# Moving the attention's projections from the first stage of a graph layer into its gather stage

## The chip, the core and the metric

One core of a Trainium2 chip runs the whole program. The metric is the device time of one execution in microseconds (us), and the time given for a kernel is the median of its runs. The engines are TensorE (PE in the profile, with PEld for its weight loads), VectorE (DVE), ScalarE (ACT), GpSimd (POOL) and SyncE (SP), which issues plain transfers.

## The reference, cut to what matters

The layer works on 6250 nodes with 256 features and 206,250 edges (100,000 in both directions and one self loop for each node). It adds a graph attention, a linear attention over all nodes and a mixture of eight experts. The linear attention is the part that the change touches:

```python
xn = _layernorm(x)                                   # (6250, 256)
# linear attention: rmsnorm, projection, softmaxes, context, output
qkv = rmsnorm(xn, g_pre) @ w_qkv                     # w_qkv (256, 384)
q, k, v = to_heads(split(qkv))                       # 4 heads of 32 features
k = concatenate([mem_kv[0], k]); v = concatenate([mem_kv[1], v])
q = softmax(q, over the features of a head) * SCALE
k = softmax(k, over all nodes)
context = einsum('bhdn,bhen->bhde', k, v)
out = einsum('bhde,bhdn->bhen', context, q)
mix = rmsnorm(out @ w_out + b_out, g_out) + xn
# graph attention: x@W; e = exp(leaky(el[src] + er[dst])); sums over src of e * (x@W)[dst]
gnn = elu(sums / rowsums + b)
x = x + gnn + mix
x = x + moe(_layernorm(x))                           # 8 experts, two of them weighted for each node
```

Since the softmax of the keys runs over all nodes, the context (128 by 128, by heads) is ready only when every node has been projected, and the outputs of the linear attention can follow only after it.

## The kernel before

The nodes are cut into 49 tiles of 128 rows (`NT`), in 13 groups of four (`groups`; the last group has one tile). All data are float32 unless said.

**First stage.** For each group `project(t0, n)` loads the rows (`xt`), takes mean and variance on ACT, normalises (`xn`, L338), transposes the tile on PE (`tp`, L343), copies it back on ACT (`xT`, L345) and multiplies it with `wcat`, which holds the columns for q, k, v and for the graph table side by side, 456 in all (L348, output `pr`). ACT then copies q out into `q_all` (L351), k and v into `kv` (L352) and 72 columns into `tab` (L355); these go to the graph table in DRAM (`table`). Behind each group stand three calls of `sort_batch`, of 51 in all, which sort the edges by source. A batch counts on PE (`n_ps`, L395), scans on DVE (L399), makes ranks on PE (`r_ps`, L419 and L420), reads them with a reduction on DVE (L427), builds one-hot rows on DVE (`ohp`, L448; `rv`, L444) and multiplies them on PE (`g_ps`, L454).

When the projections are done, `context()` runs between the remaining batches: one reduction on DVE over all keys finds the maximum (`kmax`, L468), POOL subtracts it from the keys (L498), ACT takes the exponentials (L499), and PE sums keys times values over 49 tiles (L502). At its end stands `cw`, the context times `w_out`.

**Gather stage.** `pack(q)` makes, for two tiles at a time, the list of edge targets in order (`dst_x`, L951; its heavy steps are `ohc` L923, `rc` L930, `ohp` L935 on DVE and `s_ps` L940 on PE). For each tile `gather` then issues 35 indirect transfers on POOL (L972), each of 128 table rows, into one of three buffers `xe`. A tile's gather may start when the tile three before it has been summed. The sums are `weights` (`z`, L1018 to L1029; exponentials `ew`, L1031) and four calls of `sums`, each with one wide product on DVE (`ohw`, L1041) and some eleven matmuls on PE (`a_ps`, L1048). `look` prepares the one-hot rows of the next tile (L984, L997, ACT copy `ohT` L1001, L1009).

Other work is placed between these by a list `todo` of generators with a cost for each of their steps, of which `some_more` takes a share four times a tile. At first the list holds the outputs of the linear attention, 39 steps for 13 groups, at two units a step:

```python
todo = [(attention(), [FC] * (3 * len(groups)))]        # FC = 2
```

In `attention()` each group takes the softmax of q (DVE L583, L584, L586 to L588, ACT L585), then for each tile a transpose on PE (L594), a copy on ACT (L596), a matmul with `cw` (256 columns, L598), an addition on DVE (L599) and a square on ACT (L601); at last the norm, a second load of `x` and the sum, stored to `base_y` in DRAM (L603 to L620). A block's four calls of a tile take at most two units each, so the 39 steps are spread over the first ten tiles. When they are done the experts' weights are loaded, and each block of four tiles that has been summed puts its `finish_steps` on the list: L681 to L764 and the experts, `h_ps` (512 columns, L775), Gelu (L783), `y_ps` (256 columns, L791) and the weighted sum on DVE (L795).

Within these bounds the order of each engine's instructions is fixed when the program is built, by a scheduler that follows the program's order and the buffers; each engine works its list in order. `later(ins)` ties an instruction behind the first `dst_x`, so that it is not moved ahead of it. In the gather stage PE's outputs other than the sums share two PSUM buffers (`y_ps`) and one of 512 columns (`h_ps`).

Of the kernel before, what the change touches and what calls it, by code (L numbers as in the profile page):

```python
# [1 line left out]

# [15 lines left out]
P = 128  # L18
# [17 lines left out]
def tile_gps_layer(  # L36
# [53 lines left out]
    KW = 2 * HID + 1  # L90
    O_TAB = 3 * HID
    O_EL = O_TAB + H + FO
    PW = O_EL + H
    assert NPAD > N and PW <= 512 and last > 0
# [141 lines left out]
    with tc.tile_pool(name="ids", bufs=1) as lp:  # L236
# [21 lines left out]
    nc.scalar.dma_start(out=wcat[:, :, :3 * HID], in_=w_qkv.rearrange("(c p) f -> p c f", p=P))  # L258
    nc.scalar.dma_start(
        out=wcat[:, :, O_TAB + H:O_EL], in_=gnn_W.rearrange("(c p) f -> p c f", p=P)  # L260
    )
# [3 lines left out]
    gpre = kp.tile([P, DC], F32, name="gpre")  # L265
# [5 lines left out]
    wo = kp.tile([P, D], F32, name="wo")  # L271
    nc.scalar.dma_start(out=wo, in_=w_out)
    mk = kp.tile([P, NM], F32, name="mk")
    nc.scalar.dma_start(out=mk, in_=mem_kv[0].rearrange("h d m -> (h d) m"))
    mv = kp.tile([P, NM], F32, name="mv")
# [6 lines left out]
    for c in range(DC):  # L282
        wt_ps = mps.tile([FO, P], F32, name="tp")
        nc.tensor.transpose(wt_ps, wcat[:, c, O_TAB + H:O_EL], ident)
        wT = qw.tile([FO, P], F32, name="wT")
        nc.scalar.copy(wT, wt_ps)
        wlr_ps = mps.tile([P, 2 * H], F32, name="pr")
        nc.tensor.matmul(wlr_ps, lhsT=wT, rhs=lrT, start=True, stop=True)
        nc.scalar.copy(wcat[:, c, O_TAB:O_TAB + H], wlr_ps[:, :H])
        nc.scalar.copy(wcat[:, c, O_EL:PW], wlr_ps[:, H:])  # L290
        nc.vector.tensor_scalar(
            wcat[:, c, :3 * HID], wcat[:, c, :3 * HID], gpre[:, c:c + 1], None, op0=OP.mult
        )

    q_all = qp.tile([P, NT, HID], F32, name="q_all")
    kv = kp.tile([P, NT, KW], F32, name="kv")
    nc.gpsimd.memset(kv[:, :, KW - 1:KW], 1.0)
    kmax = kp.tile([P, HID], F32, name="kmax")

    def xn_of():  # L300
        return qw.tile([P, D], F32, name="xn")

    def project(t0, n):
# [10 lines left out]
        for j in range(n):  # L314
# [8 lines left out]
        rn = qw.tile([P, GT], F32, name="rn")  # L323
        nc.scalar.activation(rn[:, :n], var, AF.Sqrt, scale=float(D))
        nc.vector.tensor_mul(rn[:, :n], rn[:, :n], rs)
        nc.vector.tensor_scalar_max(rn[:, :n], rn[:, :n], 1e-12)
        nc.vector.reciprocal(rn[:, :n], rn[:, :n])
        nc.vector.tensor_scalar_mul(rn[:, :n], rn[:, :n], float(D) ** 0.5)
        shift = qw.tile([P, GT], F32, name="shift")
        nc.vector.scalar_tensor_tensor(  # L330
            shift[:, :n], stats[:, t0:t0 + n, 0], -1.0, rs, op0=OP.mult, op1=OP.mult
# [3 lines left out]
        for j in range(n):  # L335
# [3 lines left out]
                xn, xt[:, j, :], AF.Identity, bias=shift[:, j:j + 1], scale=rstd[:, t:t + 1]  # L339
# [7 lines left out]
            for c in range(DC):  # L347
# [3 lines left out]
            nc.scalar.activation(q_all[:, t, :], pr[:, :HID], AF.Copy, scale=rn[:, j:j + 1])  # L351
            nc.scalar.activation(  # L352
                kv[:, t, :2 * HID], pr[:, HID:3 * HID], AF.Copy, scale=rn[:, j:j + 1]
            )
            nc.scalar.copy(tab[:, j, :], pr[:, O_TAB:PW])  # L355
# [110 lines left out]

    def context():
        nc.vector.tensor_reduce(  # L468
            kmax, kv[:, :NT - 1, :HID].rearrange("p t d -> p d t"), axis=AX.X, op=OP.max
        )  # L470
        nc.vector.tensor_max(kmax[:last], kmax[:last], kv[:last, NT - 1, :HID])
        km_ps = mps.tile([HID, P], F32, name="tp")
        nc.tensor.transpose(km_ps, kmax, ident)
        kcol = kp.tile([P, 2], F32, name="kcol")
        nc.vector.tensor_reduce(kcol[:, 0:1], km_ps, axis=AX.X, op=OP.max)
        nc.vector.tensor_reduce(kcol[:, 1:2], mk, axis=AX.X, op=OP.max)
        kmc = kp.tile([P, 1], F32, name="kmc")
        nc.vector.tensor_max(kmc, kcol[:, 0:1], kcol[:, 1:2])
        kr_ps = mps.tile([P, HID], F32, name="tp")
        nc.tensor.transpose(kr_ps, kmc.to_broadcast([P, P]), ident)  # L480
        krow = kp.tile([P, HID], F32, name="krow")
        nc.vector.tensor_copy(krow, kr_ps)
        nkm = kp.tile([P, 1], F32, name="nkm")
        nc.vector.tensor_scalar_mul(nkm, kmc, -1.0)
        emk = kp.tile([P, NM], F32, name="emk")
        nc.scalar.activation(emk, mk, AF.Exp, bias=nkm)
        mm_ps = mps.tile([NM, 2, P], F32, name="tp")
        nc.tensor.transpose(mm_ps[:, 0, :], emk, ident)
        nc.tensor.transpose(mm_ps[:, 1, :], mv, ident)
        memT = kp.tile([NM, 2, P + 1], F32, name="memT")  # L490
        nc.vector.memset(memT, 1.0)
        nc.vector.tensor_copy(memT[:, :, :P], mm_ps)
        ctx_ps = mps.tile([P, HID + 1], F32, name="pr")
        nc.tensor.matmul(ctx_ps, lhsT=memT[:, 0, :P], rhs=memT[:, 1, :], start=True, stop=False)
        yield
        for t0, n in groups:
            kk = kv[:, t0:t0 + n, :HID]
            nc.gpsimd.tensor_sub(kk, kk, krow[:, None, :].to_broadcast([P, n, HID]))  # L498
            nc.scalar.activation(kk, kk, AF.Exp)  # L499
            for t in range(t0, t0 + n):  # L500
                rows = P if t < NT - 1 else last
                nc.tensor.matmul(  # L502
                    ctx_ps, lhsT=kv[:rows, t, :HID], rhs=kv[:rows, t, HID:KW],
                    start=False, stop=(t == NT - 1),
                )
            yield
        rden = kp.tile([P, 1], F32, name="rden")
        nc.vector.reciprocal(rden, ctx_ps[:, HID:HID + 1])
        nc.vector.tensor_scalar_mul(rden, rden, float(DH) ** -0.5)
        cbd = kp.tile([P, HID], F32, name="cbd")  # L510
        nc.vector.memset(cbd, 0.0)
        for h in range(MH):
            s = slice(h * DH, (h + 1) * DH)
            nc.vector.tensor_scalar(cbd[s, s], ctx_ps[s, s], rden[s], None, op0=OP.mult)
        cT_ps = mps.tile([P, HID], F32, name="tp")
        nc.tensor.transpose(cT_ps, cbd, ident)
        cT = kp.tile([P, HID], F32, name="cT")
        nc.scalar.copy(cT, cT_ps)
        cw_ps = mps.tile([P, D], F32, name="pr")
        nc.tensor.matmul(cw_ps, lhsT=cT, rhs=wo, start=True, stop=True)  # L520
        nc.scalar.copy(cw, cw_ps)
        yield

# [20 lines left out]
    steps = context()  # L544
    while batches:
        sort_batch(batches.pop(0))
        next(steps, None)
    for _ in steps:
        pass
# [17 lines left out]
    def later(ins):  # L567

        tc.add_manual_dep(
            ins.ins, gate[0].ins.name,  # L570
            mybir.DependencyInfo(mybir.DependencyClass.NoSync, mybir.DependencyReason.DATA),
        )

    def attention():
# [4 lines left out]
        for t0, n in groups:  # L579
# [10 lines left out]
            o_g = qw.tile([P, GT, D], F32, name="o_g")  # L590
            ss = qw.tile([P, GT], F32, name="ss")
            for j in range(n):
# [7 lines left out]
                sq = qw.tile([P, D], F32, name="sq")  # L600
# [455 lines left out]
    todo = [(attention(), [FC] * (3 * len(groups)))]  # L1056
# [207 lines left out]
```

## Time and profile before

| | |
|---|---|
| median of 3 runs | 4222.5 us (4214.7 to 4229.85) |
| profiled execution, its own time | 4182.5 us |
| its span | 4180.7 us |
| busy in the span: PE, PEld, DVE, ACT, POOL | 54%, 40%, 46%, 18%, 40% |
| mean granted clock of TensorE | 0.711 |
| first gather issued, last gather issued | 446.2 us, 3993.6 us |
| gathers of one tile (35 indirect transfers) | 44 us on POOL, tile after tile, 49 tiles |

The profile is of one execution, and its times are counted from the start of the span. In a row of the windows view the first pair is the window, then its length, then for each engine the busy time and in brackets the number of instructions, then the granted clock of TensorE as a share of full speed, the busy share of the DMA engines and their rate. In a row of a group the first number behind the bar is the busy time, the second the mean of one instruction in ns; overlapping matmuls make the busy time less than count times mean. Behind "<-" stands what ended a wait. "Remote" means that the profile knows a semaphore's wait but not the instruction that ended it.

### The profile page before, as it was taken

The page shows a single profiled execution, that of the slowest core. Times are in us where ns is not written, and L with a number is a line of the kernel's source. Part 1 is how long each engine was busy: PE and PEld are TensorE (multiplying, and loading weights), DVE is VectorE, ACT ScalarE, POOL GpSimd, SP SyncE. Part 2 cuts the span into 40 slices and gives each one's busy share as a digit, 9 for nine tenths or more (in the row PEclk, how much of TensorE's full clock was granted, in tenths as well). Part 3 has the DMA queues.
Part 4 walks back from the last instruction along what each step waited for, and adds up shares of the span by engine and source line. Part 5 has one row for each costly group of instructions (what it writes and reads, how often), then busy time and mean ns, then how long its engine had stood idle before and what let it go on. Part 6 is the DMA issues. An engine that isn't in the chain of part 4 may idle for free. (4 is left out here: it accounts for less than half of the span.)

```text
span 4180.7 us, 39357 instructions
## 1 busy us (share of the span) xinstructions
PE 2268.6 (54%) x15401; PEld 1663.9 (40%) x15401; DVE 1919.8 (46%) x3941; ACT 746.2 (18%) x1653; POOL 1669.8 (40%) x1774
## 2 busy tenths in 40 slices
PE   7877232435254764644765555455364573554677
PEld 4544232324242543433543433334253352442456
DVE  7787444536352443533442523425343452342423
ACT  5542001212111111111111110111111111110122
POOL 1001545454445344344344344544535335344410
PEclk8875555666666877776877776777676686776778
DMA  1020111111121111011011100101101001011100
GB/s 59 28 29 1 21 28 41 37 41 37 34 74 20 22 19 23 18 24 22 12 29 18 25 17 17 30 17 22 25 12 27 18 19 25 13 25 19 23 12 7
DMA packets 106548, 103.75 MB, mean 25 GB/s; under 512 B 42678, under 2 KB 78740, under 8 KB 106356
## 3 DMA queue, kind: packets, MB, share of 16 engines
q0 software_dynamic: 54720, 60.52, 8.4%
q1 hardware_dynamic: 49940, 39.75, 3.3%
q8 instruction: 123, 2.02, 0.2%
q10 hardware_dynamic: 1696, 0.89, 0.1%
q14 instruction: 69, 0.57, 0.0%
HBM read 86.39 MB, written 14.65 MB: 24 GB/s over the span
## 5 line engine op out<-in xcount | busy, mean ns | idle before, releaser
L972 POOL DMA_INDIRECT xe<-table,dst_x x1710 | 1635.7, 957 | 2011.0 <-PE a_ps L1048 1323.2
L1048 PE MATMUL a_ps<-ohw,xe 128*65 128x128 f32 x4400 | 665.1, 307 | 235.7 <-issue 189.3
L1048 PEld LDWEIGHTS a_ps<-ohw,xe 128*65 128x65 f32 x4400 | 590.8, 159 | 314.4 <-issue 243.1
L775 PE MATMUL h_ps<-tokT,w1s 128*128 128x512 f32 (+3 forms) x896 | 442.8, 610 | 235.1 <-ACT hT L783 205.1
L795 DVE SCALAR_TENSOR_TENSOR x<-y_ps,comb,x 128x256 f32<-128x256 f32 x392 | 187.0, 481 | 782.4 <-remote 479.1
L791 PE MATMUL y_ps<-w2s,hT 128*128 128x256 f32 x1568 | 436.7, 413 | 147.6 <-issue 107.2
L791 PEld LDWEIGHTS y_ps<-w2s,hT 128*128 128x128 f32 x1568 | 315.5, 208 | 273.0 <-issue 177.5
L940 PE MATMUL s_ps<-rc,ohp 128*128 128x144 f16 x2525 | 255.1, 260 | 279.5 <-DVE ohp L935 146.8
L1041 DVE TENSOR_TENSOR ohw<-oh,bank 128x1280 f32<-128x1280 bf16 x196 | 321.5, 1641 | 170.1 <-remote 149.3
L940 PEld LDWEIGHTS <-ohp 128*128 128x128 f16 x2525 | 209.6, 114 | 324.2 <-DVE ohp L935 162.9
L1009 PE MATMUL e_ps<-elw,ohT 128*128 128x48 bf16 x588 | 36.2, 199 | 544.7 <-ACT ohT L1001 477.8
L783 ACT ACTIVATE hT<-h_ps,b1s 128x512 f32<-128x512 f32 (+3 forms) x224 | 140.4, 627 | 1018.4 <-remote 531.0
L775 PEld LDWEIGHTS h_ps<-tokT,w1s 128*128 128x128 f32 x896 | 171.8, 214 | 345.7 <-ACT hT L783 226.0
L1001 ACT COPY ohT<-t_ps 128x768 bf16<-128x768 bf16 x98 | 78.3, 799 | 1130.1 <-remote 842.3
L930 DVE TENSOR_TENSOR rc<-ohc,bank 128x1152 f16<-128x1152 f16 (+1 forms) x350 | 231.2, 687 | 64.8 <-remote 62.2
L1009 PEld LDWEIGHTS <-ohT 128*128 128x128 bf16 x588 | 27.0, 106 | 577.2 <-ACT ohT L1001 505.9
L935 DVE TENSOR_TENSOR ohp<-to,bank 128x2048 f16<-128x2048 f16 (+1 forms) x175 | 193.5, 1105 | 0.0
L763 PE MATMUL y_ps<-b2s,cTs 8*128 8x256 f32 x98 | 49.7, 600 | 192.4 <-ACT cTs L761 118.6
L764 DVE TENSOR_TENSOR x<-x,y_ps 128x256 f32<-128x256 f32 x49 | 20.6, 420 | 269.7 <-remote 164.6
L1018 DVE TENSOR_REDUCE z<-e_ps 128x140 f32<-128x420 f32 (+1 forms) x49 | 28.7, 585 | 244.6 <-PE e_ps L1009 224.1
L923 DVE TENSOR_TENSOR ohc<-to,bank 128x1152 f16<-128x1152 f16 (+1 forms) x175 | 119.6, 683 | 0.3 <-ACT to L911 0.2
L448 DVE TENSOR_TENSOR ohp<-rank,iota_h 128x4096 f16<-128x4096 f16 (+1 forms) x51 | 116.1, 2277 | 6.3 <-ACT rank L439 6.0
(273 smaller groups left out, 2568.0 us busy)
## 6 DMA issues: line engine op xcount, KB each, us to landing
xe<-table,dst_x POOLq DMA_INDIRECT x1710
xt<-in_x_dram SPq DMA_DIRECT2D x24, 512.0 KB
base_y<-xt SPq DMA_DIRECT2D x12, 512.0 KB
yt<-base_y SPq DMA_DIRECT2D x9, 512.0 KB
out_dram<-x SPq DMA_DIRECT2D x9, 512.0 KB
w1s<-in_L_ffn_w_dram SPq DMA_DIRECT2D x8, 256.0 KB
w2s<-in_L_ffn_w_dram SPq DMA_DIRECT2D x8, 256.0 KB
table<-tab SPq DMA_DIRECT2D x12, 138.0 KB
```

The source lines that it names most:

```text
L448: nc.vector.tensor_tensor(pairs(ohp[:, :w]), two(rank2[:, :w], P // 2), row(iota_h, P // 2), op=OP.is_equal)
L775: nc.tensor.matmul(h_ps[:, :w], lhsT=w1s[:, e, c, f * P:(f + 1) * P], rhs=held["tokT"][:, c, :w], start=(c == 0), stop=(c == DC - 1),)
L783: nc.scalar.activation(held[e][:, f, :w], h_ps[:, :w], AF.Gelu, bias=b1s[:, k:k + 1])
L791: nc.tensor.matmul(y_ps, lhsT=held[e][:, f, j * P:(j + 1) * P], rhs=w2s[:, e, f, :], start=(f == 0), stop=(f == FC - 1),)
L795: results.append(nc.vector.scalar_tensor_tensor(x2[:, j, :], y_ps, held["comb"][:, j, e:e + 1], x2[:, j, :], op0=OP.mult, op1=OP.add,))
L923: nc.vector.tensor_tensor(pairs(ohc[:, :m]), twos(to[:, 0, t0:t0 + m], U * CW // 2), iota_2[:, :, :U * CW // 2].to_broadcast([P, m, U * CW ...
L930: nc.vector.tensor_tensor(pairs(rc[:, :m, i, :]), pairs(ohc[:, :m]), twos(edges_q[:, t0:t0 + m, i, :], U * CW // 2), op=OP.mult,)
L935: nc.vector.tensor_tensor(pairs(ohp[:, :m]), twos(to[:, 1, t0:t0 + m], P // 2), iota_2.to_broadcast([P, m, P // 2, 2]), op=OP.is_equal,)
L940: nc.tensor.matmul(flat(s_ps), lhsT=ohp[:, t - t0, :], rhs=flat(rc[:, t - t0]), start=(t == 0), stop=(t == NBT - 1),)
L972: nc.gpsimd.indirect_dma_start(out=xe[:, c, :], out_offset=None, in_=table, in_offset=bass.IndirectOffsetOnAxis(ap=dst_x[:, c:c + 1], axis=0),
L1041: nc.vector.tensor_tensor(ohw[:, :n], oh[:, g0:g1, i, None, :].to_broadcast([P, n, H, SN]), ew_s[:, c0:c0 + n, :, None].to_broadcast([P, n ...
L1048: nc.tensor.matmul(a_ps[:, i].rearrange("f h n -> f (h n)"), lhsT=xe[:, c, H:], rhs=ohw[:, c - c0].rearrange("p h n -> p (h n)"), start=(c ...
```

## The change

The first stage keeps only what the table needs. `wcat` shrinks to 72 columns, `project` copies out `tab` alone, and `context()` is taken out of the first stage; the sort batches that stood among its steps follow one another. What belongs to the linear attention becomes a new `context()` in the gather stage, which stands in `todo` ahead of `attention()`: 41 steps and 39 steps, each now at one unit, so that a call takes two of them.

For each group of four tiles the new `context()` loads `x` again (the load for the next group is issued one step ahead), normalises (ACT), transposes (PE) and copies back (ACT) into `xnT`, 512 nodes wide; makes the keys by feature, `k_ps` with 128 features by 512 nodes (PE); takes the group's maximum for each feature (DVE) and updates a running maximum, with a factor `shrink` for what was summed before; takes the exponentials (ACT); makes q and v by tile, 256 columns (PE, two copies on ACT); transposes the exponentials back (PE, one copy on ACT); sums keys times values of the group in PSUM and adds the sum to `sums_c` (DVE). The weights for q, k, v and a few small tensors move from the pool that is closed after the first stage into the one that stays open until the attention is done, and two buffers of `attention()` (`o_g`, `sq`) are cut to a single copy.

```diff
-    nc.scalar.dma_start(out=wcat[:, :, :3 * HID], in_=w_qkv.rearrange("(c p) f -> p c f", p=P))
+    wqvk = qp.tile([P, DC, 3, HID], F32, name="wqvk")
+    for i, k in enumerate((0, 2, 1)):
+        nc.scalar.dma_start(out=wqvk[:, :, i], in_=w_qkv[:, k * HID:(k + 1) * HID]...)
...
     def project(t0, n):
...
-        nc.vector.tensor_mul(rn[:, :n], rn[:, :n], rs)
-        nc.vector.tensor_scalar_max(rn[:, :n], rn[:, :n], 1e-12)
-        nc.vector.reciprocal(rn[:, :n], rn[:, :n])
-        nc.vector.tensor_scalar_mul(rn[:, :n], rn[:, :n], float(D) ** 0.5)
...
-            nc.scalar.activation(q_all[:, t, :], pr[:, :HID], AF.Copy, scale=rn[:, j:j + 1])
-            nc.scalar.activation(
-                kv[:, t, :2 * HID], pr[:, HID:3 * HID], AF.Copy, scale=rn[:, j:j + 1]
-            )
-            nc.scalar.copy(tab[:, j, :], pr[:, O_TAB:PW])
+            nc.scalar.copy(tab[:, j, :], pr)
...
-    steps = context()
     while batches:
         sort_batch(batches.pop(0))
-        next(steps, None)
...
+    def context():
...
+        for g, (t0, n) in enumerate(groups):
+            v = vs[g % 2]
+            xnT = qw.tile([P, DC, GT * P], F32, name="xnT", bufs=1)
+            for j in range(n):
+                t = t0 + j
+                xn = xn_of()
+                nc.scalar.activation(xn, xt[:, j, :], AF.Identity, bias=shift_all[:, t:t + 1],
+                    scale=rn_all[:, t:t + 1])
+                xT_ps = yps.tile([P, DC, P], F32, name="y_ps")
+                for c in range(DC):
+                    nc.tensor.transpose(xT_ps[:, c, :], xn[:, c * P:(c + 1) * P], ident)
+                nc.scalar.copy(xnT[:, :, j * P:(j + 1) * P], xT_ps)
+            if g + 1 < len(groups):
+                xt = load(g + 1)
+            yield
+            k_ps = hps.tile([P, GT * P], F32, name="h_ps")
+            for c in range(DC):
+                nc.tensor.matmul(k_ps[:, :w], lhsT=wqvk[:, c, 2], rhs=xnT[:, c, :w], ...)
+            here = small("here")
+            nc.vector.tensor_reduce(here, k_ps[:, :w], axis=AX.X, op=OP.max)
+            new = small("most")
+            nc.vector.tensor_max(new, most, here)
+            less = small("less")
+            nc.vector.tensor_scalar_mul(less, new, -1.0)
+            shrink = small("shrink")
+            nc.scalar.activation(shrink, most, AF.Exp, bias=less)
+            most = new
+            ekT = qw.tile([P, GT * P], F32, name="ekT", bufs=1)
+            nc.scalar.activation(ekT[:, :w], k_ps[:, :w], AF.Exp, bias=less)
+            for j in range(n):
+                qv_ps = yps.tile([P, 2, HID], F32, name="y_ps")
+                for c in range(DC):
+                    nc.tensor.matmul(flat(qv_ps), lhsT=xnT[:, c, j * P:(j + 1) * P],
+                        rhs=flat(wqvk[:, c, :2]), ...)
+                nc.scalar.copy(q_all[:, t0 + j, :], qv_ps[:, 0])
+                nc.scalar.copy(v[:, j, :HID], qv_ps[:, 1])
+            yield
+            for j in range(n):
+                nc.tensor.transpose(ek_ps[:r, j, :], ekT[:, j * P:j * P + r], ident)
+            nc.scalar.copy(ek[:r, :n], ek_ps[:r, :n])
+            for j in range(n):
+                nc.tensor.matmul(c_ps, lhsT=ek[:r, j, :], rhs=v[:r, j, :], ...)
+            nc.vector.scalar_tensor_tensor(sums_c, sums_c, shrink, c_ps, op0=OP.mult, op1=OP.add)
+            yield
...
-    todo = [(attention(), [FC] * (3 * len(groups)))]
+    todo = [(chain(context(), attention()), [1] * (6 * len(groups) + 2))]
```

## The prediction, made before the changed kernel ran

> **What bounds the kernel now.** I read the windows view first, by stage, then the waits of the gather stage, then groups and single instructions for prices.
>
> ```profile
> core 0: us, PE busy (x) PEld busy (x) DVE busy (x) ACT busy (x) POOL busy (x), PEclk, DMA share, GB/s
> 86.80:284.40 197.60, 175.35 (x2044) 103.85 (x2041) 152.87 (x252) 116.49 (x449) 2.86 (x18) 0.81 0.11 33
> 284.40:410.00 125.60, 83.48 (x1132) 57.97 (x1132) 104.66 (x128) 26.34 (x86) 19.32 (x15) 0.61 0.12 3
> 558.80:1099.00 540.20, 218.04 (x1472) 179.37 (x1470) 262.47 (x537) 79.28 (x185) 272.74 (x281) 0.64 0.17 38
> 1306.40:3893.20 2586.80, 1410.92 (x8215) 1033.72 (x8216) 1064.42 (x2268) 367.07 (x546) 1133.03 (x1190) 0.73 0.11 21
> 640.20:666.60 26.40, 0.00 (x0) 0.00 (x0) 0.00 (x0) 0.00 (x0) 15.89 (x17) 0.50 0.17 24
> ```
>
> Row 1 is the projections among 27 sort batches, row 2 the context among the last 16: PE and DVE are both nearly full. Row 3 is gather tiles 2 to 9, where the change puts its work, row 4 tiles 13 to 46. Row 5 is a piece of one tile: only POOL's gathers run, PE, DVE and ACT do nothing at all.
>
> ```profile
> POOL xe L972 <- PE a_ps L1048: 1302.9, 43, 51.4
> ```
>
> This is from the waits between 600 and 3900 us: 43 times POOL waits, 30.3 us each, until PE has summed the tile three before. So a tile is serial: 35 gathers (43.4 to 45.7 us), about 5.5 us until the other engines move again, and then what is left of the tile's work. The others get 9 to 25 us of work done early in a burst and then stand still until its end. Work added here is therefore paid, though PE is idle 60% of row 3. Tiles 2 to 9 take 67.5 us each with PE 27.3 and DVE 32.8 busy; tiles 13 to 46 take 76.1 with 41.5 and 31.3. So 8.6 us of time stand against 14.2 us more PE, 0.60 for one. A least-squares fit over tiles 3 to 47 gives 41.5 + 0.57 PE + 0.35 DVE (rms 3.8 us); with ACT as a third term 43.0 + 0.54 PE + 0.17 DVE + 0.48 ACT (rms 3.6). I use the first.
>
> **First stage: what goes.** The first gather is issued at 446.2. Sort batch starts (`ohp` L448) are at 36.6, 86.8 (8th), 284.4 (35th) and 410.0 (51st, a short one of about 3.1 us): 373.4 us in all. With projections a batch takes 197.6/27 = 7.32 us; without, 6.0 (at 300 to 324 us) to 6.92 (four batches from 378 us, clock 0.50).
>
> ```profile
> L348 PE MATMUL pr<-wcat,xT 128*128 128x456 f32 x196 | 109.8, 690 | 5.9 <-ACT xT L345 5.9
> L351 ACT ACTIVATE q_all<-pr,rn 128x128 f32<-128x128 f32 x49 | 17.8, 364 | 47.2 <-PE pr L348 47.0
> L468 DVE TENSOR_REDUCE kmax<-kv 128x128 f32<-128x6144 f32 x1 | 11.0, 11044 | 0.0
> L498 POOL TENSOR_TENSOR kv<-kv,krow 128x512 f32<-128x512 f32 x12 | 18.6, 1586 | 41.1 <-DVE krow L482 41.1
> ```
>
> These groups lie in 0 to 440 us. The 456-column matmuls become 72 columns wide: 109.8 us become about 39, bounded by their 196 weight loads at some 200 ns. ACT loses L351 (17.8) and L352 (22.9), DVE the 11.0 of `kmax`, POOL the 18.6, PE the 17.9 of L502. While POOL subtracts, DVE's L444 takes 1.25 to 1.56 us where it had taken 0.58:
>
> ```profile
> 328.58 0.58 DVE L444 TENSOR_TENSOR rv<-ob,vb 128x832 f16<-128x832 f16 x1
> 337.88 1.56 DVE L444 TENSOR_TENSOR rv<-ob,vb 128x832 f16<-128x832 f16 x1
> ```
>
> So 49 pitches plus 3.1 us: at 6.0 us 297 (76 saved), at 6.35 314 (59 saved), at 6.92 342 (31 saved). DVE alone needs 152.87/27 = 5.66. I take 6.35, between: tables and statistics still stand among three quarters of the batches, but PE falls from 6.5 us a batch to about 4. First stage: -59.
>
> **Gather stage: what comes.** Prices are from the groups between 446 and 1100 us, nearest in place and kind:
>
> ```profile
> L598 PE MATMUL y_ps<-cw,qT 128*128 128x256 f32 x82 | 37.0, 541 | 50.3 <-ACT qT L596 44.6 <-issue 4.4 <-DVE ohw L1041 0.7
> L594 PE MATMUL y_ps<-ident,q_all 128*128 128x128 f32 x41 | 13.7, 334 | 1.6 <-DVE q_all L588 1.6
> ```
>
> - PE: 147 transposes (98 of `xn`, 49 of `ekT`) at 13.7/41 = 0.334 make 49 us (36 at the first stage's 0.247); 52 k matmuls of 512 columns as L775 (442.8/896 = 0.494) 26; 196 q/v matmuls of 256 columns at 37.0/82 = 0.451 make 88 (55 at L791's 436.7/1568 = 0.279); 98 of the context at 0.185 (L502) 18. Together 181, at the low prices 135; I take 158, for PE will be busier here than now but less than where L791 stands.
> - DVE: 13 maxima of 512 columns at 0.675 (as L583) 8.8, 26 small operations at 0.17 4.4, 13 additions to `sums_c` at 0.3 3.9, beginning and end about 5: 22.
> - ACT: 49 normalisations at 0.606, 49 copies of 256 columns at 0.385, 98 of 128 columns at 0.264, 13 exponentials and 13 copies of 512 columns at about 0.6, 13 of `shrink` at 0.2: 93.
>
> Two-engine fit: 0.57·158 + 0.35·22 = 98. Three-engine fit: 0.54·158 + 0.17·22 + 0.48·93 = 134. The two first bursts have nothing to sum, so about one group of 13 (8 us) is done there for nothing: 90 and 126. I take 100, nearer the two-engine one, since ACT runs in chains with PE and is idle 85% of row 3.
>
> [...] The granted clock is 0.81 where the projections stand now (row 1), 0.64 where they go (row 3) and 0.50 in the frozen piece (row 5), and a 256-column matmul takes 0.451 us between the gathers of row 3 against 0.279 among the experts' runs. With every price at its high end the sum is 0.57·23 = 13 us above mine, with every one at its low end 13 below. [...]
>
> **What is moved or added and priced at nothing.** Attention keeps its instructions but runs in tiles 5 to 9 alone at double rate: about 13 us of DVE more a tile there, 13 less in tiles 0 to 4; the fit is linear, so the sum is zero. If the lighter tiles can't fall as the heavier ones rise, it costs up to 5·13·0.35 = 23. From about tile 11 on the order of every engine's instructions is as before. Thirteen more loads of `x` (512 KB, on SP's queue among attention's loads and stores, one step ahead) are 6.3 MB; SP's queue moved 39.75 MB in 3.3% of the span, so they take about 22 us of the engines' time, in some 330 us at a DMA share of 0.17; uncovered at most 22. POOL's queue holds the same gathers and loses only the subtractions. New waits: DVE's maximum waits for PE's k, and behind it in DVE's list stand `pack`'s steps and `z`; ACT's copies wait for PE's transposes, and behind them stand `ohT` and `ew`; transposes, q/v and sums all take turns in the two `y_ps` buffers, each freed only by a copy on ACT or DVE. If each of 39 steps holds up a tile's chain by 0.5 us, that is 20; zero if the next tile's `ohw` waits anyway. This is inside 90 to 126.
>
> **Sum.** -59 + 100 = +41. The profiled execution took 4182.5 us (span 4180.7), which gives 4223.5. The median of 4222.5 is 40 above the profiled time, so the same step on it gives 4263.5, rounded to 4263. A difference of 0.3% (13 us) is about what a measurement of this kernel can tell from no change.
>
> **Rivals.**
> - *Faster, 4182 (0.20).* PE's idle time takes the work. For: PE is idle 322 of 540 us in row 3, and the early part of a burst has 9 to 25 us in which engines do run; bursts 0 to 2 have little to sum. If gather growth is 20 us and the first stage gives 61, -41. It decides where growth over the ten tiles stays under about 59 us, 6 a tile: at the fit's 0.57 some 70 of the 158 us on PE (41/0.57) would have to be hidden beyond what the fit hides already. Against: row 5, and the 30.3 us wait that ends with PE.
> - *Much slower, 4317 (0.20).* With less PE work in the first stage its clock stays at 0.50 and the pitch at 6.92 (-31), while ACT and PE exchange halves at each step so that the three-engine fit holds (+126): +95. For: the four 6.92 batches stand where no context is left. Against: their POOL and table work is different from the earlier batches'.
> - *No difference, near 4222 (0.10).* Growth equals saving, say 65 against 65.
> - That the change doesn't do what it says can be left out: in the new order of PE's instructions 24 of 98 transposes and 16 q/v matmuls stand among the first tile's sums, and no 456-column matmul is left.
>
> **Numbers.** Likeliest 0.50 of slower by 20 to 70; with the much slower case that makes slower by over 0.3% 0.70, within 0.3% 0.10, faster by over 0.3% 0.20. The likeliest case's own range is 4235 to 4290 (pitch 6.0 to 6.6, growth 85 to 115). The whole range, leaving a tenth at each end, is 4190 to 4325: half of the faster case lies below it, and half of the much slower one, 8 us of waits on top of it, above.
>
> **What the changed profile would show.** The first gather issued near 387 us (right if 370 to 415; if over 415, the pitch is the failed step). Batches at about 6.35 us with DVE busy 5.7 of it. Tiles 2 to 4 and 5 to 9 at about 75 to 80 us instead of 67.5, their PE busy 16 us higher, clock 0.64 or more. Tiles from 13 on at 76 as before. The context's matmuls should lie mostly between the end of a burst and the next one's start; if they lie early in bursts and POOL's wait for L1048 stays 30 us or less, the faster rival is right. If the late waits name DVE's maximum or SP's loads, my zero prices were wrong.

## The result and the profile after

The changed kernel took 4253.8 us in the median of five runs (4248.44 to 4262.45), the kernel before 4217.86 in five (4211.72 to 4229.85): 36 us slower, ratio 1.0083 (95% interval 1.0061 to 1.0106). The forecast was 4263 with a range of 4190 to 4325. It was right in its sign and near in its size, but both terms of its sum were wrong, and their errors made up for each other.

The profiled execution of the changed kernel has a span of 4248.0 us, 67.3 more than that of before; the execution of before was one 35 us under its median. By stages, in us:

| | before, recorded | after, recorded | difference | before, profiled again | wide (below) | difference |
|---|---|---|---|---|---|---|
| first gather issued | 446.2 | 420.1 | -26.1 | 443.9 | 419.7 | -24.2 |
| gathers of tiles 0 to 12 | 860.1 | 916.9 | +56.8 | 858.9 | 907.1 | +48.2 |
| tiles 13 to 25 | 1012.0 | 1028.5 | +16.5 | 1012.9 | 1026.4 | +13.5 |
| tiles 26 to 46 | 1574.9 | 1589.3 | +14.4 | 1570.7 | 1573.2 | +2.5 |
| last two tiles and the end | 287.5 | 293.2 | +5.7 | 291.3 | 289.9 | -1.4 |

The right half is from executions on one chip, "wide" being the changed kernel with wider matmuls in the first stage, which moved nothing there; its sum, 38.6, is near the 36 that the medians show. The 14.4 and 5.7 of the left half, where the right half has 2.5 and -1.4, are then mostly not the program's.

The windows view of the changed kernel, stage by stage (batches among the projections, the last 16 batches, tiles 2 to 9, tiles 13 to 46; what the clock of 1.00 in the first two rows means stands under wide):

```profile
core 0: us, PE busy (x) PEld busy (x) DVE busy (x) ACT busy (x) POOL busy (x), PEclk, DMA share, GB/s
84.00:286.10 202.10, 169.59 (x2052) 116.27 (x2052) 148.99 (x206) 93.77 (x375) 8.66 (x18) 1.00 0.10 29
286.10:383.90 97.80, 67.20 (x1025) 42.15 (x1026) 86.30 (x119) 16.76 (x68) 1.17 (x2) 1.00 0.17 8
535.20:1122.80 587.60, 291.93 (x1912) 231.75 (x1912) 266.48 (x561) 127.05 (x365) 269.69 (x281) 0.70 0.19 38
1337.00:3954.70 2617.70, 1430.80 (x8235) 1042.89 (x8236) 1069.63 (x2289) 372.46 (x553) 1130.95 (x1190) 0.73 0.13 20
```

Row 1 is 27 batches: 7.49 us each, where I had put 6.35 and where the kernel before had 7.32; PE, which I had put at about 4 us a batch, is busy 6.28 of it (6.49 before). Row 2 is 16 batches at 6.11 (125.6 us before, 97.8 now): all of the first stage's saving lies here, where the context was. In row 3 tiles 2 to 9 take 73.5 us each in place of 67.5, with PE 36.5 busy in place of 27.3. POOL still waits for the sums, 32.5 us a time (the waits between 600 and 3900 us):

```profile
POOL xe L1023 <- PE a_ps L1099: 1364.2, 42, 48.5
```

The groups of the context on PE, from the first gather to the gather of tile 13 (420.1 to 1337.0 us), beside the prices that I had used:

```profile
L584 PE MATMUL y_ps<-wqvk,xnT 128*128 128x256 f32 x196 | 59.4, 444 | 82.1 <-remote 39.7 <-ACT v L589 39.5 <-issue 1.9
L566 PE MATMUL h_ps<-xnT,wqvk 128*128 128x512 f32 x48 | 27.1, 674 | 1.1 <-issue 0.8 <-ACT xnT L559 0.3
L558 PE MATMUL y_ps<-ident,xn 128*128 128x128 f32 x98 | 22.2, 318 | 36.4 <-ACT xn L552 33.5 <-ACT xnT L559 1.0 <-issue 0.9
L601 PE MATMUL y_ps<-v,ek 128*128 128x129 f32 x96 | 17.0, 323 | 4.5 <-ACT ek L598 3.7 <-ACT v L589 0.7
L595 PE MATMUL y_ps<-ident,ekT 128*128 128x128 f32 x48 | 8.7, 312 | 13.6 <-remote 7.0 <-ACT ekT L580 6.6
```

They sum to 134, with the last group's short ones 136, where I had taken 158.

### The profile page after: what moved, and what is told of

It reads as the page before. It is cut to its first block, busy times and chain, and to the rows that moved or that the text cites. A ratio compares the mean times of both kernels' runs of the same rounds, so it can differ in the third digit from the quotient of the medians.

```text
span 4248.0 us, 40359 instructions
## 1 busy us (share of the span) xinstructions
PE 2347.7 (55%) x15794; PEld 1735.4 (41%) x15794; DVE 1915.7 (45%) x3946; ACT 766.6 (18%) x1763; POOL 1653.4 (39%) x1760
## 4 chain that ended last, share of the span: by engine, by line
another core or an unknown queue 28%; PE 27%; DVE 6%; issue 5%; ACT 3%; DVEq 0%; ACTq 0%
PE y_ps L842 8%; PE a_ps L1099 7%; PE h_ps L826 7%; PE s_ps L991 2%; PE y_ps L814 1%; DVE ohw L1092 1%; ACT hT L834 1%; PE y_ps L763 1%; DVE ohp L986 1%; ACT ohT L1052 1%; DVE inc L944 0%; DVE x L846 0%; DVE rc L981 0%; PE t_ps L1048 0%
## 5 line engine op out<-in xcount | busy, mean ns | idle before, releaser
L1099 PE MATMUL a_ps<-ohw,xe 128*65 128x128 f32 x4400 | 638.4, 300 | 158.4 <-DVE ohw L1092 88.7
L1099 PEld LDWEIGHTS a_ps<-ohw,xe 128*65 128x65 f32 x4400 | 573.5, 155 | 222.5 <-DVE ohw L1092 104.3
L1060 PEld LDWEIGHTS <-ohT 128*128 128x128 bf16 x588 | 27.1, 103 | 453.7 <-ACT ohT L1052 344.3
L437 DVE TENSOR_TENSOR ohp<-rank,iota_h 128x4096 f16<-128x4096 f16 (+1 forms) x51 | 115.2, 2259 | 14.4 <-ACT rank L428 14.4
```

The costliest lines, as they stand in the source:

```text
L1099: nc.tensor.matmul(a_ps[:, i].rearrange("f h n -> f (h n)"), lhsT=xe[:, c, H:], rhs=ohw[:, c - c0].rearrange("p h n -> p (h n)"), start=(c ...
```

## The experiments

**Two kinds of executions.** The runs below fell on more than one chip, and on them the same program behaves in two ways; without this the numbers can't be read. In one kind, that of the recorded profiles, the engines stand still for much of each tile's gathers, and the kernel before takes 4180 to 4230 us. In the other they work on, and it takes 2739 to 2749. before_again, wide, noctx and bf16 are of the standing kind (the kernel before took 4185.71 beside them), all others of the free kind (2742.28 and 2743.43). The first four fell on one chip, the others on two more; whether the chip makes the kind is not shown beyond that.

**before_again.** The kernel before, unchanged.

> The kernel before, unchanged, profiled a second time. Between the two profiled executions 67 us lie, between the medians 36: the gather stage from tile 13 on, whose instructions are the same, took 2586.8 us before and 2617.7 after, 30.9 more, and the first execution of before was 35 us under the median of its runs. Theory 1 (that execution was an uncommonly short one): a second profile shows tiles 13 to 46 at 2605 to 2625 us and the whole near 4218, with the first gather again near 446 and tiles 0 to 12 again near 860. Theory 2 (the changed kernel really loses 31 us after tile 13): tiles 13 to 46 at 2587 again, the whole near 4185.

Measured: span 4177.7 us, first gather 443.9, tiles 0 to 12 858.9, tiles 13 to 46 2583.6; the kernel before took 4185.71 beside it. So the recorded profile is no short execution by chance: on this chip 4180 is usual, and theory 1 falls in that form. The changed kernel does lose something after tile 13, 16 us of the 31 by the table's right half; the other 15 are not seen on this chip.

**wide.** The 456-column matmul back in the first stage.

```diff
-                    pr, lhsT=xT[:, c, :], rhs=wcat[:, c, :], ...
+                    pr, lhsT=xT[:, c, :], rhs=wide[:, c, :], ...   # 384 more columns, not read
```

> The changed kernel, with the 456-column matmul put back in the first stage (384 of its columns are computed and not read). Batches among the projections take 7.49 us in the changed kernel, 7.32 before, though TensorE has less to do; the 416-column rank matmul takes 0.52 us there, 0.37 before. Theory 1 (clock: with the wide matmuls gone TensorE falls to its slow clock, and that holds the batches): the rank matmul is back at 0.36 to 0.40 us, the pitch at 6.9 us or less, the first gather at 405 us or earlier (420.1 in the changed kernel). Theory 2 (the order of the batch's steps across PE, ACT and DVE sets the pitch, whatever the clock): pitch 7.3 to 7.6 us and first gather at 416 to 425 us, even with the rank matmul at 0.37. Theory 3 (TensorE's work counts there): pitch over 8 us, first gather at 435 us or later.

Measured: first gather at 419.7 us, pitch 7.54; span 4216.2. The windows view of the 27 batches, and the group of the rank matmul among the projections in the kernel before, in the changed kernel and in wide:

```profile
83.40:287.10 203.70, 183.64 (x2052) 105.09 (x2051) 151.00 (x212) 94.52 (x373) 6.54 (x18) 0.77 0.10 29
```

```profile
L419 PE MATMUL r_ps<-ob,upto_own 128*128 128x416 f16 x53 | 20.0, 377 | 3.7 <-DVE rank L427 3.7
```

```profile
L408 PE MATMUL r_ps<-ob,upto_own 128*128 128x416 f16 x54 | 28.5, 528 | 4.4 <-DVE rank L416 4.4
```

```profile
L410 PE MATMUL r_ps<-ob,upto_own 128*128 128x416 f16 x53 | 21.2, 400 | 1.3 <-DVE rank L418 1.3
```

With the wide matmuls the rank matmul is back at 0.400 us from 0.528, at a granted clock of 0.77, and nothing is won. Its length and PE's work changed together here: PE is busy 14 us more than in the changed kernel (183.64 against 169.59), and the pitch is the same to 0.06 us. So PE's busy time does not set the pitch, and theory 2 is left; the short rank matmul beside the narrow projections, which is what the forecast of 6.35 assumed, was not run. That the clock of this stage was lower in the changed kernel than before is read only from such durations (in nostats the same matmul took 0.519 us at a granted clock of 0.53): its PEclk column reads 1.00 there, since the trace holds no record of the clock before 419 us.

**noctx.** The gather stage without the context's groups; their 39 steps stay empty, and q is a constant.

> The changed kernel without the 13 groups of the context in the gather stage (no load, transposes, k, q, v, exponentials or sums; q is a constant; the empty steps stay, so that the attention still runs at double rate in tiles 5 to 9). From the first gather to the gather of tile 13 the changed kernel takes 916.9 us, the kernel before 860.2. Theory 1 (the growth is the context's work, paid at 0.57 of PE's time): 850 to 870 us. Theory 2 (part of it comes from the attention at double rate): 875 us or more. If the empty first tiles give back more than the attention costs, below 850.

Measured: 859.3 us from the first gather to tile 13's, as in the kernel before (858.9). So all growth of tiles 0 to 12 is the context's, its loads of `x` included. The attention at double rate moves time, as the sum had it, without adding any: tiles 2 to 6 took 306.0 in place of 334.2, tiles 7 to 12 443.1 in place of 412.8. Tiles 13 to 25, without any context before them, took 1030.8. (The first gather at 430.8 is later than in the changed kernel; the constant is written on POOL ahead of the batches, and the first batch starts at 43.6 us in place of 34.5.)

**bf16.** Rows and weights of q, k and v in bf16, in the gather stage only.

```diff
-            xnT = qw.tile([P, DC, GT * P], F32, name="xnT", bufs=1)
+            xnT = qw.tile([P, DC, GT * P], BF16, name="xnT", bufs=1)
-                wqvk[:, c], wqvk[:, c], gpre[:, c:c + 1], None, op0=OP.mult
+                wq16[:, c], wqvk[:, c], gpre[:, c:c + 1], None, op0=OP.mult
```

> The changed kernel with the normalised rows and the weights of q, k and v in bf16 in the gather stage, all else the same: 248 of the context's matmuls (59.4 us for q and v, 27.7 for k) get shorter, ACT's and DVE's instructions stay. Theory 1 (PE's time is what is paid, at 0.57): if these matmuls fall to 25 to 35 us, the stretch from the first gather to tile 13's falls by 29 to 35 us, from 917 to about 885, and the whole by as much, near 4221. Theory 2 (the chain PE, copy on ACT, PE is paid by its steps, not by the matmul's length): 10 us or less, near 4245.

Measured: 4227.97 us, ratio to before 1.0100 (1.0083 to 1.0117). The windows view from the first gather to tile 13's, of before_again, of wide (the same gather stage in float32) and of bf16:

```profile
443.90:1302.80 858.90, 332.32 (x2217) 268.03 (x2217) 403.48 (x844) 122.81 (x273) 440.52 (x456) 0.63 0.19 39
```

```profile
419.70:1326.70 907.00, 412.06 (x2697) 331.45 (x2697) 417.88 (x897) 176.82 (x491) 439.66 (x455) 0.67 0.21 44
```

```profile
420.40:1328.50 908.10, 370.19 (x2573) 303.71 (x2573) 417.19 (x897) 187.16 (x499) 438.58 (x455) 0.67 0.21 44
```

PE has 42 us less to do and the stretch is as long. The same view of tiles 2 to 6 and of tiles 7 to 12, first of wide, then of bf16:

```profile
536.40:898.90 362.50, 190.88 (x1309) 154.83 (x1307) 160.38 (x318) 86.72 (x242) 168.07 (x176) 0.73 0.17 34
898.90:1326.70 427.80, 187.99 (x1210) 153.26 (x1207) 219.40 (x493) 76.92 (x219) 205.10 (x210) 0.66 0.24 58
```

```profile
536.60:877.10 340.50, 153.15 (x1192) 129.92 (x1190) 143.48 (x282) 80.85 (x229) 166.68 (x176) 0.68 0.18 35
877.10:1328.50 451.40, 186.93 (x1204) 152.17 (x1201) 235.68 (x529) 90.56 (x232) 205.62 (x210) 0.66 0.23 55
```

Tiles 2 to 6 are 22 us shorter, tiles 7 to 12 24 us longer. But the two kernels do not have the same work there (the expectation of bf16_78 below takes it that they do): the scheduler has put the instructions in another order, and with it 16 to 17 us of DVE's work, softmax steps of the attention, have moved from tiles 2 to 6 into tiles 7 to 12. There ACT also loads its tables 21 times in place of 13, at 1.28 us each. So the 22 us are not the price of PE's time alone, and it can't be told from this run how much of the 24 us is moved work and table loads, and how much is waiting that came back later.

**after_again** and **after_third.** The changed kernel, unchanged, among the last eight runs; **before_third**, the kernel before beside the second of them.

> The changed kernel, unchanged, profiled again beside the kernels below, as the mark that they are held against. If the sum is a first stage 24 to 26 us shorter, tiles 0 to 12 45 to 57 us longer and tiles 13 to 25 15 us longer, whatever the chip, the first gather is at 419 to 421 us, tiles 0 to 12 take 907 to 917 us, tiles 13 to 25 1026 to 1029.

> The kernel before, profiled beside the three below. The executions seen so far are of two kinds: in one the engines stand still in the later part of every tile's gathers and the kernel before takes 4180 to 4220 us, in the other they work through the gathers, gathers follow one another without a gap (0.3 us), and it took 2742. If this is of the first kind: first gather near 444, tiles 0 to 12 near 859, tiles 13 to 25 near 1012, the whole 4180 to 4220. If it is of the second: gathers without gaps in this kernel too, 44 to 46 us a tile, first gather near 444 and the whole near 2742.

> The changed kernel, timed beside the kernel before. Theory 1 (added work in the gather stage costs only what the standing still leaves no room for): in the kind with standing engines 30 to 45 us slower than before, with the first gather 24 to 26 earlier, tiles 0 to 12 45 to 57 longer, tiles 13 to 25 15 longer; in the other kind the gather stage is as long as before to 8 us and the change is 16 to 24 us faster, the first stage's saving. Theory 2 (the added work costs the same in both): slower in both.

Measured: 2724.86 us (before: 2742.28), then 2718.18 (before: 2743.43), ratio 0.9906 (0.9889 to 0.9922) for the second. Here the change is 17 and 25 us **faster** (the 17 from a single execution of the changed kernel). The windows view from the first gather to tile 13's and over the 34 tiles after it, of before_third and then of after_third:

```profile
446.60:1035.00 588.40, 328.67 (x2403) 268.48 (x2404) 425.80 (x897) 131.78 (x287) 449.68 (x455) 0.73 0.29 57
1035.00:2541.70 1506.70, 1242.32 (x8214) 959.69 (x8212) 1062.01 (x2262) 366.75 (x542) 1143.83 (x1191) 0.89 0.22 36
```

```profile
420.20:1005.50 585.30, 409.70 (x2906) 327.17 (x2907) 443.81 (x969) 187.70 (x509) 446.63 (x456) 0.83 0.32 68
1005.50:2512.40 1506.90, 1241.87 (x8212) 958.22 (x8210) 1061.74 (x2264) 369.02 (x545) 1144.25 (x1191) 0.89 0.22 36
```

The same 81 us more of PE's work, which cost 48 to 57 us in the standing kind, cost nothing here: 585.3 against 588.4. That is theory 1. POOL no longer waits for the sums. Its largest entries in after_third's waits, from the first gather to tile 47's, are its own issue (0.3 us at most) and the first gather's wait for its list:

```profile
POOL xe L1023 <- issue: 487.6, 1600, 0.3
POOL xe L1023 <- DVE loc L1010: 124.4, 2, 124.1
```

And the first stage saves 26.4 us here too (446.6 to 420.2). One tile shows the difference. The windows view of tile 20's gathers in the recorded changed kernel, the first 15 us and the other 28.4, then the same of after_third:

```profile
1899.10:1914.10 15.00, 10.48 (x64) 7.51 (x62) 8.70 (x13) 1.72 (x3) 11.34 (x13) 0.99 0.17 27
1914.10:1942.50 28.40, 7.68 (x26) 4.48 (x26) 3.88 (x6) 0.00 (x0) 21.67 (x23) 0.50 0.19 28
```

```profile
1315.40:1330.40 15.00, 11.93 (x33) 6.56 (x33) 9.65 (x35) 5.02 (x9) 11.36 (x12) 0.61 0.25 30
1330.40:1358.80 28.40, 28.40 (x167) 20.37 (x166) 15.39 (x40) 5.25 (x10) 21.65 (x23) 0.95 0.18 29
```

POOL's work is the same (21.67 and 21.65 us); in the one PE does 7.68 us of work in the later part and ACT none, in the other PE is busy without a gap.

**units78** and **units78_again.** Two `yield`s taken out, so that the list has 78 units.

```diff
         xt = load(0)
-        yield
...
         nc.scalar.copy(cw, cw_ps)
-        yield
```

> The changed kernel with two of its 80 steps merged into their neighbours, so that the list holds 78 units, as before, and the experts' steps begin in the same call as before. From tile 13 to 25 the changed kernel's instructions stand in another order than before (from tile 26 on in the same), and these 13 tiles took 1012 us before and 1027 to 1031 in every kernel with 80 units, also in the one without the context. Theory 1 (the two units push the experts' steps one call on, and that order costs 15 us): tiles 13 to 25 at 1010 to 1015 us, their order as before, the whole 10 to 18 us shorter than the changed kernel, unless tiles 0 to 12 are reordered for the worse. Theory 2 (the 15 us are carried over from the longer tiles before, or from the memory traffic): 1024 us or more.

> The changed kernel with 78 units on the list in place of 80, as before. With standing engines: tiles 13 to 25 at 1010 to 1015 us in place of 1026 to 1029, and the whole 10 to 18 us shorter than the changed kernel if tiles 0 to 12 are no worse ordered; if tiles 13 to 25 stay at 1024 or more, the order of the experts' steps is not the cause. Without: within 8 us of the changed kernel.

Measured: 2718.34 and 2719.32 us, against 2724.86 and 2718.18 of the changed kernel: no difference, as expected where gathers hide it. Tiles 13 to 25 took 576 to 578 us in all these kernels. Both runs fell on the free kind, so the question that they were made for stays open. What the traces do show: in the kernel before, 964 of the sums' matmuls (L1048) stand ahead of the first expert matmul, in the changed kernel 990, in units78 966. A call of `sums` is some 22, so the experts begin one call later in the changed kernel. That this order costs the 15 us of tiles 13 to 25 fits with the four kernels of 80 units (1026 to 1031, noctx among them), but it was not tried apart.

**bf16_78.** units78 and bf16 together.

> units78 with the normalised rows and the weights of q, k and v in bf16. With standing engines the bf16 kernel had 42 us less PE work in tiles 0 to 12, was 22 us shorter than the wide kernel in tiles 2 to 6 and 24 us longer in tiles 7 to 12, where its instructions are the same ones in another order. Theory 1 (PE's time in the context's tiles is paid at about a half, and the 24 us were an accident of order): tiles 2 to 6 again 15 to 25 us shorter than in the changed kernel, tiles 7 to 12 within 10 of it. Theory 2 (what PE gives up comes back as waits): tiles 0 to 12 together within 8 us of units78. Without standing engines: within 8 us of units78.

Measured: 2720.08 us, ratio 0.9914 (0.9898 to 0.9931); within 1 us of units78, in the free kind, where PE's time in these tiles isn't paid. It tells nothing on the 24 us above.

**bound.** The context stays in the first stage, without a maximum over the nodes: the exponentials are shifted by one number worked out from the weights, and taken while the keys are read.

```diff
-            nc.scalar.activation(kv[:, t, :2 * HID], pr[:, HID:3 * HID], AF.Copy, scale=rn...)
+            nc.scalar.activation(ek[:, j, :], pr[:, HID:2 * HID], AF.Exp, scale=rn..., bias=nkb)
+            nc.scalar.activation(v[:, j, :HID], pr[:, 2 * HID:3 * HID], AF.Copy, scale=rn...)
+            nc.tensor.matmul(ctx_ps, lhsT=ek[:r, j, :], rhs=v[:r, j, :], start=False, ...)
```

> The kernel before with its projections left in the first stage, but the context summed there by group: the shift of the keys' exponentials is one number known from the weights (16 times the largest norm of a key column, or the largest memory key), so that no maximum over the nodes is needed, and the exponentials are taken while the keys are read from PSUM. It removes the reduction over all keys, the subtraction on POOL and the second pass over keys and values behind the projections, and leaves the gather stage as before. Theory 1 (the batches' pitch among the projections is not held by PE's or ACT's amount of work, and the saving of the first stage came from taking context out of the last 16 batches): pitch among the projections 7.2 to 7.6 us, the last 16 at 6.0 to 6.2, first gather at 415 to 425 us, gather stage as before, the whole 20 to 30 us shorter than before. Theory 2 (the 98 matmuls and 26 loads of ACT's tables among the projections are paid): pitch over 8 us, first gather at 440 or later, no gain.

Measured: 2733.16 us, ratio 0.9965 (0.9951 to 0.9979), first gather at 434.3. Between the two theories: about 12 us of the hoped 25 are won, since the batches got slower, 7.63 us among the projections and 6.47 after (where five tiles are still projected, against one before). ACT is busy there 150.93 of 205.9 us (93.77 of 202.1 in the changed kernel), among it 21 loads of its tables at 1.28 us, for Exp and Sqrt in turn. It beats the kernel before and, in the free kind, not the changed one; in the standing kind, where its untouched gather stage would count, it was not run.

**nostats.** The changed kernel with mean 0 and variance 1 written in place of the passes that take them.

> The changed kernel without the passes that take mean and variance in the first stage (mean 0 and variance 1 are written instead), which are 98 of ACT's activations there with 98 reads of the sums, about 64 us of ACT's 118 among the projections; PE's and DVE's work stay. Among the projections a batch takes 7.49 us with DVE busy 5.5, PE 6.3 and ACT 3.5; wider matmuls did not change it. Theory 1 (the batch's steps on ACT, rank and the copies of g_ps, stand in line behind the projections' steps): pitch down to 6.0 to 6.6 us, first gather at 385 to 405 us. Theory 2 (order and buffers between DVE and PE alone): pitch 7.2 us or more, first gather at 412 or later.

Measured: first gather 406.1 us, 16 earlier than after_again's 422.2, between the two theories and nearer to the first. The scheduler has drawn the projections forward: 31 of the 49 tiles are projected ahead of the eighth batch, 12 in after_again. So the stretch from the eighth batch to the 35th, at 6.46 us a batch, holds half as many projections and can't be held against 7.49. From the first batch to the 35th both have nearly all of them; the windows view of that stretch, of after_again and then of nostats:

```profile
36.60:288.20 251.60, 209.88 (x2544) 143.74 (x2543) 187.00 (x258) 118.20 (x474) 10.34 (x22) 1.00 0.10 30
```

```profile
36.60:272.80 236.20, 192.93 (x2531) 131.78 (x2531) 185.20 (x237) 72.40 (x260) 5.29 (x22) 0.57 0.10 30
```

The batches take 6.95 us in place of 7.40, with the rank matmul still at 0.519 us. The edit takes work from ACT alone, so ACT's work counts in the pitch: about 64 us less of it are worth 16, at a granted clock of 0.57. Through which chain is not shown; PE, with nearly the same matmuls, is busy 17 us less too. DVE's waits for PE in this stretch fall from 49.5 us to 24.4, but its wait for ACT's `rank` rises from 13.9 to 28.5, which theory 1 does not say. Nor does ACT's busy time alone explain the pitch, for the changed kernel has 23 us less of it than the kernel before (93.77 against 116.49) and its batches are no faster. bound goes the other way, with slower batches at more work on ACT, but there PE has 9 us more too.

## Why the prediction was right, and where it was not

**First stage, -59 forecast, -24 to -26 measured.** The step that failed is the pitch of 6.35 among the projections, which I took because "PE falls from 6.5 us a batch to about 4". The last 16 batches did what was said (6.11). The other 27 did not get faster, and the step fails twice. PE's time fell to 6.28 only: the 72-column matmuls took 0.279 us each (40.2/144) where I had put 0.2, and the rank matmul 0.528 in place of 0.377. (The 4 was also summed wrongly: I took off the saving of all 49 tiles, but row 1 holds 36, which gives about 4.6.) And PE's time does not set the pitch: in wide it was 6.80 us a batch at a pitch of 7.54. ACT's work counts (nostats), but what holds the 27 batches is not settled. I had read "PE and DVE are both nearly full" out of rows in which DVE has 77% of the first and PE 66% of the second, and not looked at who waits: the waits of before name DVE's `rv` behind PE for 33.7 us and `ob` for 8.7 of 197.6, no more. The range's lower end (31 saved) lay just off the measurement. My sign, "if over 415, the pitch is the failed step", was the right one.

**Gather stage, +100 forecast, +48 to +57 measured in tiles 0 to 12.** The mis-sized term is PE's 158. The groups sum to 136, about the forecast's sum at its low prices (135), as q and v cost 59.4 in place of 88 and the transposes 31 in place of 49. And PE's busy time in the stretch rose by only 80 to 84, since matmuls overlap (all groups sum to 472 us in the changed kernel, where PE is busy 413, and to 364 in the kernel before, where it is busy 328) and the old ones got shorter. The group of the sums, before and after:

```profile
L1048 PE MATMUL a_ps<-ohw,xe 128*65 128x128 f32 x990 | 173.9, 335 | 97.5 <-issue 69.8 <-DVE ohw L1041 21.6 <-DMA xe<-table,dst_x 4.8
L1099 PE MATMUL a_ps<-ohw,xe 128*65 128x128 f32 x990 | 149.9, 303 | 53.9 <-issue 44.9 <-DVE ohw L1092 9.0
```

PE's granted clock in tiles 2 to 9 was 0.70 in place of 0.64. With PE 84 and DVE 15 the fit gives 0.57·84 + 0.35·15 = 53, and 57 was measured; with the pair on one chip, 80 and 14.4, it gives 51 against 48. (This is without the 8 us that the forecast took off for the first bursts.) So the fit came near here and its input was wrong. The three-engine fit would have given, with ACT's 54, 0.54·84 + 0.17·15 + 0.48·54 = 74. ACT's 93 was right as a sum of groups (they sum to 93), but its busy time rose by 54 only, in part because 14 loads of its tables, at 1.28 us each, stand in the stretch in place of 30. Bf16 warns against reading the fit as a law: with 42 us less on PE and another order, nothing was gained. One price was misread without harm: the 0.494 for a k matmul is the mean of L775's four widths, and its 512-column ones alone have 322.8/576 = 0.560; 0.565 was measured (27.1/48).

The signs for the gathers hold in part. Of the context's 131 us on PE in the changed kernel (overlapping matmuls counted once) 76 lay between the gathers of two tiles, 36 in the first 15 us of a tile's gathers and 20 later in them.

The high end of the prices, 13 us above my sum, was the wrong way: the groups came to 136 us where it had 181, and the sums' matmuls took 303 ns with the context among them (308 in wide), against 335 in the kernel before. How PE's work and its clock go together is not settled by these runs. In the first stage the rank matmul went from 0.377 us to 0.528 where work left, though PE was still busy 84% of that stretch; but from the first gather to tile 13's the granted clock reads 0.63 in before_again, 0.69 in noctx, without the context, and 0.67 in wide, with it. And where the rank matmul was back at 0.400 us, in wide, nothing was won.

**"From about tile 11 on the order of every engine's instructions is as before"** was wrong. The order is the same only from tile 26; tiles 13 to 25 lost 13 to 18 us in every kernel with 80 units of the standing kind. The forecast had not followed the 40th call to what stands behind it.

**The zeros that held.** The attention's double rate (noctx: 859.3 against 858.9), the 13 loads, and the waits on SP and `here`: none stands among the long waits that release POOL. In the changed kernel's waits from the first gather to tile 13's these are, beside the list for the first gather and POOL's own issue:

```profile
POOL xe L1023 <- PE a_ps L1099: 288.5, 10, 35.1
POOL xe L1023 <- PE y_ps L645: 27.4, 1, 27.4
POOL xe L1023 <- DVE dst_x L1002: 27.0, 1, 27.0
```

The last two have their like in the kernel before (57.8 and 24.9 us). noctx leaves out the context's loads together with its work, so their price was not measured alone.

**The sum.** -24 + 48 + 16 - 1 = +39 against the forecast's -59 + 100 = +41. Being near is the work of errors of opposite sign: 35 us too much saved, 52 too much paid, and 16 not seen. The rival "faster" was not far-fetched: its condition, growth under 59 us in the ten tiles, was met (48 to 57 even in thirteen), and it failed because the first stage gave less than half of what both cases had put, and tiles 13 to 25 took 15 us on top. In the free kind its mechanism, PE's idle time taking the work, is seen by itself, and it wins by 17 to 25 us.

## What to carry to other kernels

Before moving work out of a stage, find who waits in that stage, not who is busy: with PE busy 84 to 90% of the time, 14 us more of it did not move the batches, and with ACT busy 46%, about 64 us less gave 16. A price fitted over the kernel's own stages (here 0.57 us for each us of PE) came near once and failed once, and the work put into it has to be the rise in busy time (80 to 84 us here), not the sum of the groups (136). And where work is placed by counted units, two units more shifted the order of the thirteen tiles behind them.

## What the runs showed of the hardware that was not expected

The kernel before ran in 4180 to 4230 us or in 2739 to 2749, the changed one in 4248 to 4262 or in 2716 to 2725, each chip that is on record showing one kind only. A tile's 35 gathers take the same time in both (43.4 to 47.6 us). But in the slower kind PE, DVE and ACT are all three idle for 52% of the gathers' time in the kernel before and 53% in the changed one (tiles 3 to 47), in the other kind for 10 and 8%. (In a single tile of the kernel before it is 27 to 70%, so it is not always the full stop until the end that the forecast describes.) Most of this idle time lies behind the first 18 us of a tile's gathers and reaches to some 5 us after their end. What holds the engines is not shown: many of the waits there name a semaphore without an instruction that ends late ("remote"). The change's sign depends on it, +0.8% in the one kind and -0.9% in the other, so its result holds only for the kind of execution that it was measured in.

In the changed kernel's profile a granted clock of 1.00 stands where the trace holds no record of it, up to 419 us: among the projections the rank matmul took 0.528 us under that reading, 0.519 in nostats, where the column reads 0.53, and 0.377 to 0.400 in kernels where it read 0.77 to 0.81.
